# Two halves of the array's rows, a shared two-bank PSUM tile and earlier inputs in the edge networks of a graph kernel

## Chip, cores and metric

One Trainium2 chip; the kernel is one program on one of its cores. The metric is device time in microseconds (us) of one execution; lower is better. Engines are named as in the profile: PE (TensorE, matrix products into PSUM), PEld (its weight loads), DVE (VectorE), ACT (ScalarE), POOL (GpSimd, here mostly indirect DMAs), SP (issues DMAs).

## The reference

Two graph layers run one after the other on 6250 nodes of 160 values (64 scalars and 32 vectors of three) and 200000 edges, sorted by destination. Each layer is followed by a residual addition and a layer norm. Per edge a small network gives weights, which multiply the features of the edge's source node and the edge's own four values; the products are summed at the destination. Layer 1 (`i == 0` in the kernel):

```python
weight = silu(edge_attr_10 @ W_fc1) @ W_fc2          # 10 -> 100 -> 192 per edge
w0, w1, w2, w3 = weight[:, :64], weight[:, 64:128], weight[:, 128:160], weight[:, 160:]
gs, gv = x1s[src], x1v[src]                           # gathered source nodes
mid0a = w0 * gs * e_s
mid0b = w3 * (einsum('euc,ec->eu', gv, e_v) / SQRT3)
mid1a = w1[:, :, None] * gs[:, :, None] * e_v[:, None, :]
mid1b = w2[:, :, None] * gv * e_s[:, :, None]
agg = segment_sum(concatenate([mid0a, mid0b, mid1a, mid1b]), dst, n) / 4
```

Layer 2 (`i == 1`) is of the same kind: `hid = silu(edge_attr_64 @ fc_w1 / 8)` (64 -> 64), `w = hid @ fc_w2 / 8` (64 -> 224), five products instead of four, the same sum by destination, then linear mixes, gates and the norm. All is float32.

## The kernel before

**Tiles, units, chunks.** The 200000 edges are 1563 tiles of 128 edges (edges on partitions). Four tiles are a unit (391 of them), two tiles a pair. Because the edges are sorted, consecutive tiles fall into a narrow window of nodes: `plan()` makes 284 groups of 3 to 12 tiles whose destinations lie within 32 nodes (W).

**One unit** of `windows(i, ...)`, called once per layer, goes through these steps at different times:

- `gather(p)`: POOL gathers the source rows of the layer's node table by indirect DMA, one per tile (L665), four units ahead, into tile `g` (8 buffers of a pair).
- `inputs(c)`: SP loads the edge attributes of a chunk, features on partitions. In layer 1 a chunk is one unit: 10 partitions by 512 edges (L598) into one of three tiles `e0`, `e1`, `e2` that were zeroed once, so that a product may read all 128 partitions. In layer 2 a chunk is two units, and the 512 edges of a unit stand as two blocks of 64 partitions by 256 edges, one under the other (L607), in tile `e` (2 buffers). An input is asked for where the first product needs it in program order; SP's queue runs ahead as far as the buffers allow.
- `hidden(u)`: the first product of the edge network into PSUM tile `pa` (one buffer of one bank), then Silu by ACT into tile `h` in SBUF. Layer 1: one product, 128 rows by 100 columns of weights, 512 edges streamed (L623, L624). Layer 2: `fc1[1]` holds the 64x64 weights twice on the diagonal, so one product streams 256 columns for 512 edges (L634, L636).
- `weights(p)`: the second product, per tile, into `pw` (three banks, a pair in each): layer 1 with 100 rows, layer 2 with 64 rows, the upper half for the unit's first pair and the lower half for its second (L656). Pair by pair.
- `places(p)`: DVE makes the selection matrices `sel` (node in the window equals the edge's destination, times the four edge values; L699). `products(p)`: DVE multiplies `pw` with `g` into `mid` (L681, L686).
- `aggregate(t)`: six (layer 1) or seven (layer 2) products with `sel` as weights sum the tile's edges into `pg` (two banks, one per group in work), in the four 32-column tiles of the array (L723). At a group's end ACT copies `pg` to `r` (L728, L730).
- `turn(g)`: a unit later TensorE turns `r` into PSUM tile `pt` (one bank; L737 to L744), and DVE adds `pt` into the running sums `sm` (L749) and `sr` (L751) at the window's offset, which it reads from a table (L746).

**Order.** The loop at L783 writes out, for step u: gather(u+4), weights(u+2), hidden(u+3), places and products(u+2), then aggregate for the four tiles of u, then turn for the groups that ended in step u-1, then a piece of the node work (`second_nodes`, `last_nodes`, in PSUM tile `pn`). TensorE's products keep this program order (`keep_in_program_order`, helpers at L134 and L139, whose lines stand for all products in the profile); other engines' queues are ordered by the scheduler, which also sets the semaphores from the tiles that instructions read and write. `issue_after` ties the offset's read to the last DVE selection.

**PSUM.** All eight banks are used: pw 3, pg 2, pa 1, pn 1, pt 1. The prologue (`turn_nodes`, `send_nodes`, `checked`) borrows the same tiles. `general()` is a branch for inputs that aren't as the plan expects; it doesn't run here.

A float32 product appears in the profile as two LDWEIGHTS and two MATMUL instructions.

Of the kernel before, what the change touches and what calls it, by code (L numbers as in the profile page):

```python
# [81 lines left out]
def edges_of(t):  # L82
    return min(P, E - t * P)
# [3 lines left out]
def kernel(ctx: ExitStack, tc: tile.TileContext, a, out):  # L87
# [25 lines left out]

    tail_n, tail_e = N - (NB - 1) * P, E - (NT - 1) * P
# [85 lines left out]
    nc.gpsimd.dma_start(fc1[0][:10], a["W_fc1"])  # L200
# [115 lines left out]
    def checked():  # L316
        p = psum.tile([P, 512], F32, name="pa", bufs=1)
# [228 lines left out]
    def windows(i, loads, work):  # L546
# [13 lines left out]
        ec = (EC // 2, EC)[i]  # L560

        inputs_of = None
        if i == 0:

            inputs_of = [loads.tile([P, EC * P // 2], F32, name=f"e{k}", bufs=1) for k in range(3)]
            for e in inputs_of:
                nc.vector.memset(e, 0.0)
# [24 lines left out]
        def inputs(c):  # L592

            e0 = c * ec * P
            n = min(ec * P, E - e0)
            if i == 0:
                e = inputs_of[c % 3]
                nc.sync.dma_start(e[:10, :n], a["e10"][:, e0:e0 + n])  # L598
            else:

                e = loads.tile([P, EC * P // 2], F32, name="e", bufs=2)
                for u in range(0, n, 4 * P):
                    for h in range(2):
                        r = u + h * 2 * P
                        m = min(2 * P, n - r)
                        if m > 0:
                            nc.sync.dma_start(e[h * 64:h * 64 + 64, u // 2:u // 2 + m],  # L607
                                              a["e64"][:, e0 + r:e0 + r + m])
            made["e", c] = e

        def hidden(u):

            t0 = 4 * u
            c = t0 // ec
            if ("e", c) not in made:
                inputs(c)
            e = made["e", c]
            n = min(4 * P, E - t0 * P)
            p = psum.tile([P, 512], F32, name="pa", bufs=1)
            h = work.tile([P, 512], F32, name="h", bufs=2)  # L620
            at = (t0 % ec) * P
            if i == 0:
                matmul(p[:100, :n], fc1[0], e[:, at:at + n], start=True, stop=True)  # L623
                nc.scalar.activation(h[:100, :n], p[:100, :n], AF.Silu)  # L624
            else:
                at //= 2
                k = P if n > 2 * P else 64
                m = min(n, 2 * P)
# [4 lines left out]
                for kk, c0, c1 in parts:  # L633
                    matmul(p[:kk, c0:c1], fc1[1][:kk, :kk], e[:kk, at + c0:at + c1],  # L634
                                     start=True, stop=True)
# [3 lines left out]
        def weights(p):  # L639

            pw = psum.tile([P, 512], F32, name="pw", bufs=3)
            q = pw.rearrange("p (j d) -> p j d", j=2)
            h = made["h", p // 2]
            for j in range(2):
                t = 2 * p + j
                if t >= NT:
                    break
                n = edges_of(t)
                if i == 0:
                    l = h[:100, (t % 4) * P:(t % 4) * P + n]  # L650
                    r = fc2[0]
                else:
                    k = 64 * (p % 2)
                    l = h[k:k + 64, j * P:j * P + n]
                    r = fc2[1][k:k + 64, :]
                matmul(q[:n, j, :nw], l, r, start=True, stop=True)  # L656
            made["w", p] = q
# [75 lines left out]
        def turn(g):  # L733
            r = made["r", g]
            pt = psum.tile([P, 512], F32, name="pt", bufs=1)
# [47 lines left out]
        for u in range(-4, units + 1):  # L783
# [6 lines left out]
            if 0 <= u + 2 < units:  # L790
                for p in pairs_of(u + 2):
                    weights(p)
# [26 lines left out]
    def general(i, loads, work):  # L819
# [18 lines left out]
        def body(t, n):  # L838
# [20 lines left out]
            ph = psum.tile([P, 512], F32, name="pa", bufs=1)  # L859
# [7 lines left out]
            pr = psum.tile([P, 512], F32, name="pa", bufs=1)  # L867
# [122 lines left out]
```

## Time and profile before

| | |
|---|---|
| median of 8 runs | 6534.62 us (6483.35 to 6542.86) |
| the profiled execution: its own time | 6519.48 us |
| its span, first to last instruction | 6517.7 us |
| mean granted TensorE clock | 0.767 |
| PE / PEld instructions | 53817 / 53817 |
| layer 1's edge loop, first to last pw product | about 74 to 3277 us |
| layer 2's edge loop | about 3306 to 6495 us |

The costliest groups touched by the change, from the page's list (count, busy us, mean ns of one, idle time of the engine before it and what ended most of that):

| group | count | busy us | mean ns | idle before |
|---|---|---|---|---|
| POOL gathers, L665 | 3126 | 3014.7 | 964 | 3433.7, most for DVE mid |
| PE pg (sums) | 40638 | 1733.4 | 272 | 830.8, most "issue" |
| PE pw (second products) | 6252 | 1575.8 | 456 | 146.2 |
| PE pa (first products) | 1566 | 928.6 | 683 | 17.4 |
| ACT Silu, layer 1 (L624) | 391 | 232.8 | 595 | 1335.3 |
| ACT Silu, layer 2 (L636) | 392 | 150.1 | 383 | 1616.4 |
| DVE adds into sm (L749) | 568 | 162.7 | 287 | 1183.1 |

How to read it: busy time is a union of an engine's instructions, so overlapping products count once. "Issue" is time in which the engine waited for nothing that the profile shows. The chain of waits follows the last instruction back through whatever released each step. The granted clock is what the throttle let TensorE have; in this trace each piece of it is either 1.0 or 0.5.

### The profile page before, as it was taken

The numbers are of one execution on the slowest core, as the hardware profiler recorded it, in microseconds if no ns is written. First come the engines' busy times: TensorE is split into PE (matmuls) and PEld (weight loads), VectorE is DVE, ScalarE is ACT, GpSimd is POOL, SyncE is SP. The second block draws the span as 40 slices with busy tenths as digits, with TensorE's granted clock in tenths as the row PEclk, the third lists the DMA queues.
The fourth block names the chain that finished last, engine by engine and source line by source line (L and its number), as shares of the span: only waits on it lengthen the run. The fifth ranks groups of instructions, "written<-read, shape, count | busy, mean of one in ns | idle before, by whom it ended". The sixth has DMA issues, their size and how long they took to land.

```text
span 6517.7 us, 137335 instructions
## 1 busy us (share of the span) xinstructions
PE 4854.0 (74%) x53817; PEld 3253.8 (50%) x53817; DVE 2937.9 (45%) x10845; ACT 947.4 (15%) x2386; POOL 3036.3 (47%) x3232
## 2 busy tenths in 40 slices
PE   6787777777777777777767777777777777776766
PEld 4455555555555555555544444444444454444544
DVE  5544444444444444334344444444444444544444
ACT  1111111111111122111110000101111111111112
POOL 4555555444444344333345555555444444444443
PEclk8888888887887788777677777777777777777667
DMA  3222222222222122111122222222222222222221
GB/s 98 51 54 54 53 55 54 51 51 51 51 52 52 45 51 51 44 41 45 42 55 64 64 63 66 65 65 66 64 63 62 64 65 64 66 59 58 54 59 45
DMA packets 301526, 371.47 MB, mean 57 GB/s; under 512 B 86988, under 2 KB 245213, under 8 KB 300873
## 3 DMA queue, kind: packets, MB, share of 16 engines
q0 software_dynamic: 151056, 257.36, 16.3%
q1 hardware_dynamic: 121192, 88.36, 5.2%
q10 hardware_dynamic: 28624, 16.88, 0.9%
q8 instruction: 430, 7.05, 0.5%
q14 instruction: 224, 1.83, 0.1%
HBM read 341.49 MB, written 20.80 MB: 56 GB/s over the span
## 4 chain that ended last, share of the span: by engine, by line
PE 71%; issue 18%; another core or an unknown queue 5%; DVE 4%; ACT 1%; DVEq 0%; DMA 0%; SPq 0%; ACTq 0%
PE pg L134 24%; PE pw L134 23%; PE pa L134 12%; PE pn L134 7%; PE pt L139 4%; DVE sel L699 1%; PE pt L134 1%; DVE mid L686 1%; PE pn L139 1%; DVE mid L681 1%; DVE sm L749 0%; DVEq L746 0%; DVE nx L442 0%; DVE sr L751 0%
## 5 line engine op out<-in xcount | busy, mean ns | idle before, releaser
L665 POOL DMA_INDIRECT g<-table,src x3126 | 3014.7, 964 | 3433.7 <-DVE mid L686 2044.1
L134 PE MATMUL pg<-mid,sel 128*32 128x32 f32 (+3 forms) x40638 | 1733.4, 272 | 830.8 <-issue 813.9
L134 PEld LDWEIGHTS pg<-mid,sel 128*32 128x32 f32 x40638 | 1198.4, 127 | 1787.0 <-issue 1767.7
L134 PE MATMUL pw<-fc,h 100*128 100x192 f32 (+1 forms) x6252 | 1575.8, 456 | 146.2 <-issue 115.2
L699 DVE SCALAR_TENSOR_TENSOR sel<-iota,off,ea 128x128 f32<-128x128 f32 x3126 | 958.4, 344 | 1441.0 <-remote 494.7
L134 PEld LDWEIGHTS pw<-fc,h 100*128 100x128 f32 (+1 forms) x6252 | 1153.5, 248 | 353.5 <-issue 257.9
L686 DVE TENSOR_TENSOR mid<-g,pw 128x192 f32<-128x192 f32 x3910 | 1167.4, 345 | 0.0
L134 PE MATMUL pa<-e,fc 128*100 128x512 f32 (+1 forms) x1566 | 928.6, 683 | 17.4 <-issue 10.3
L681 DVE TENSOR_TENSOR mid<-pw,g 128x256 f32<-128x256 f32 x1564 | 654.3, 418 | 597.6 <-PE pw L134 351.4
L749 DVE TENSOR_TENSOR sm<-pt,sm 96x128 f32 (+1 forms) x568 | 162.7, 287 | 1183.1 <-PE pt L139 650.2
L134 PEld LDWEIGHTS pa<-e,fc 128*100 128x100 f32 (+1 forms) x1566 | 328.9, 236 | 198.6 <-issue 190.6
L624 ACT ACTIVATE h<-pa 100x512 f32<-100x512 f32 x391 | 232.8, 595 | 1335.3 <-PE pa L134 1012.0
L728 ACT ACTIVATE r<-pg 128x96 f32<-128x96 f32 (+1 forms) x568 | 156.4, 275 | 1616.3 <-remote 623.1
L636 ACT ACTIVATE h<-pa 128x256 f32<-128x256 f32 x392 | 150.1, 383 | 1616.4 <-PE pa L134 1494.4
L139 PE MATMUL pt<-ident,r 128*96 128x128 f32 (+1 forms) x852 | 247.0, 310 | 101.6 <-DVE sr L751 56.0
L134 PE MATMUL pn<-rm,sm 96*128 96x128 f32 (+4 forms) x980 | 224.6, 400 | 107.7 <-DVE sm L749 93.3
L134 PE MATMUL pt<-ident,r 128*32 128x32 f32 x2272 | 151.3, 219 | 177.9 <-issue 122.8
L134 PEld LDWEIGHTS pn<-rm,sm 96*128 96x128 f32 (+3 forms) x980 | 215.0, 288 | 122.1 <-DVE sm L749 97.4
L134 PEld LDWEIGHTS pt<-ident,r 128*32 128x32 f32 x2272 | 111.1, 125 | 219.5 <-issue 176.7
L139 PEld LDWEIGHTS pt<-ident,r 128*96 128x96 f32 (+1 forms) x852 | 111.4, 131 | 204.0 <-issue 104.4
L139 PE MATMUL pn<-ident,nx 128*128 128x128 f32 (+1 forms) x196 | 50.6, 348 | 140.0 <-DVE nx L442 140.0
L134 PE MATMUL pn<-rr,sr 64*128 64x128 f32 (+2 forms) x196 | 79.7, 502 | 65.9 <-DVE sr L751 57.2
(132 smaller groups left out, 1359.7 us busy)
## 6 DMA issues: line engine op xcount, KB each, us to landing
g<-table,src POOLq DMA_INDIRECT x3126
e<-in_e SPq DMA_DIRECT2D x781, 64.0 KB
e<-in_e SPq DMA_DIRECT2D x390, 20.0 KB
ea<-in_ea_main SPq DMA_DIRECT2D x63, 96.0 KB
xself<-no ACTq DMA_DIRECT2D x48, 96.0 KB
no<-xself SPq DMA_DIRECT2D x48, 96.0 KB
xg<-in_x_main SPq DMA_DIRECT2D x12, 320.0 KB
table<-rg SPq DMA_DIRECT2D x12, 320.0 KB
```

The source lines that it names most:

```text
L134: r = nc.tensor.matmul(*args, **kw)
L139: r = nc.tensor.transpose(*args)
L624: nc.scalar.activation(h[:100, :n], p[:100, :n], AF.Silu)
L636: nc.scalar.activation(h[:kk, c0:c1], p[:kk, c0:c1], AF.Silu, scale=0.125)
L665: nc.gpsimd.indirect_dma_start(out=g[:n, j, :], out_offset=None, in_=table[i][:, :], in_offset=bass.IndirectOffsetOnAxis(ap=of(t)[0], axis=0))
L681: nc.vector.tensor_tensor(two, q[:n, :m, 0:2 * S].rearrange("p j (k d) -> p j k d", k=2), gs, OP.mult)
L686: nc.vector.tensor_tensor(o[:, :, at:at + 96].rearrange("p j (c d) -> p j c d", c=3), gv, q[:n, :m, None, w0:w0 + V].to_broadcast([n, m, 3 ...
L699: made["last"] = nc.vector.scalar_tensor_tensor(s[:n, j], iota[:n, None, :].to_broadcast([n, 4, W]), w, e[:, :, None].to_broadcast([n, 4, ...
L728: nc.scalar.activation(r[:, :w], pg[:, :w], AF.Copy)
L749: nc.vector.tensor_tensor(sm[:h, :, at], pt[:h, :P].rearrange("p (c w) -> p c w", c=4), sm[:h, :, at], OP.add)
```

## The change

- **Layer 1's first products** become two: the unit's edges stand as two blocks of 10 partitions by 256 edges, at partitions 0 and 64, as in layer 2. `fc1[0]` holds the 10 rows of weights at both places, and each half of 64 rows multiplies its own block into its own bank. ACT then runs two Silu.
- **Layer 2's second products** are issued alternately from the unit's two pairs (`weights(ps)` takes both pairs at once), so that the row halves alternate. Layer 1 keeps its order; both pairs' PSUM tiles are taken before the first product.
- **One PSUM tile `pair`** of two banks, made once, replaces pa and pt. Columns 0 to 255 of the banks hold first products (layer 1: both banks; layer 2: bank `u % 2`); columns 256 to 511 of bank `g % 2` hold the turned sums of group g. The prologue's uses of pa and pt go to its two banks.
- **Inputs**: both layers use chunks of two units and the same three zeroed tiles, now made outside `windows`; `hidden` asks for its own chunk and the next. Layer 1's full chunks are loaded by one transfer per half.

```diff
+    pair = psum.tile([P, 2, 512], F32, name="pair", bufs=1)
...
-    nc.gpsimd.dma_start(fc1[0][:10], a["W_fc1"])
+    for r in (0, 64):
+        nc.gpsimd.dma_start(fc1[0][r:r + 10], a["W_fc1"])
...
-        z = psum.tile([P, 512], F32, name="pa", bufs=1)
+        z = pair[:, 0, 0:P]
...
-            tag, k = (("pg", 2), ("pn", 1), ("pg", 2), ("pt", 1))[j]
-            p = psum.tile([P, 512], F32, name=tag, bufs=k)
+            tag, k = (("pg", 2), ("pn", 1), ("pg", 2), (None, 0))[j]
+            p = psum.tile([P, 512], F32, name=tag, bufs=k) if tag else pair[:, 1]
...
         def inputs(c):
...
+            e0 = c * EC * P
+            n = min(EC * P, E - e0)
+            k, of_e = ((10, a["e10"]), (64, a["e64"]))[i]
+            e = inputs_of[c % 3]
+
+            for h in range(2):
+                if i == 0 and n == EC * P:
+                    nc.sync.dma_start(
+                        e[h * 64:h * 64 + k].rearrange("p (u m) -> p u m", m=2 * P),
+                        of_e[:, e0:e0 + n].rearrange("p (u h m) -> p u h m", h=2, m=2 * P)[:, :, h])
+                    continue
                 for u in range(0, n, 4 * P):
...
         def hidden(u):
 
             t0 = 4 * u
-            c = t0 // ec
-            if ("e", c) not in made:
-                inputs(c)
+            c = t0 // EC
+            for k in (c, c + 1):
+                if ("e", k) not in made and k * EC < NT:
+                    inputs(k)
             e = made["e", c]
             n = min(4 * P, E - t0 * P)
-            p = psum.tile([P, 512], F32, name="pa", bufs=1)
             h = work.tile([P, 512], F32, name="h", bufs=2)
-            at = (t0 % ec) * P
+            at = (t0 % EC) * P // 2
+            m = min(n, 2 * P)
             if i == 0:
-                matmul(p[:100, :n], fc1[0], e[:, at:at + n], start=True, stop=True)
-                nc.scalar.activation(h[:100, :n], p[:100, :n], AF.Silu)
+
+                halves = [(0, m)] + [(1, n - m)] * (n > m)
+                for j, m in halves:
+                    k = slice(64 * j, 64 * j + 64)
+                    matmul(pair[:100, j, :m], fc1[0][k], e[k, at:at + m], start=True, stop=True)
+                for j, m in halves:
+                    nc.scalar.activation(h[:100, 2 * P * j:2 * P * j + m], pair[:100, j, :m], AF.Silu)
             else:
-                at //= 2
+                p = pair[:, u % 2]
...
-        def weights(p):
-
-            pw = psum.tile([P, 512], F32, name="pw", bufs=3)
...
+        def weights(ps):
+
+            for p in ps:
+                pw = psum.tile([P, 512], F32, name="pw", bufs=3)
+                made["w", p] = pw.rearrange("p (j d) -> p j d", j=2)
+
+            for p, j in [(p, j) for p in ps for j in range(2)] if i == 0 else \
+                    [(p, j) for j in range(2) for p in ps]:
                 t = 2 * p + j
...
+                if t < NT:
+                    h, n = made["h", p // 2], edges_of(t)
+                    if i == 0:
+                        l, r = h[:100, (t % 4) * P:(t % 4) * P + n], fc2[0]
+                    else:
+                        k = slice(64 * (p % 2), 64 * (p % 2) + 64)
+                        l, r = h[k, j * P:j * P + n], fc2[1][k]
+                    matmul(made["w", p][:n, j, :nw], l, r, start=True, stop=True)
...
         def turn(g):
             r = made["r", g]
-            pt = psum.tile([P, 512], F32, name="pt", bufs=1)
+            pt = pair[:, g % 2, 2 * P:]
...
             if 0 <= u + 2 < units:
-                for p in pairs_of(u + 2):
-                    weights(p)
+                weights(pairs_of(u + 2))
...
+            inputs_of = [loads.tile([P, EC * P // 2], F32, name=f"e{k}", bufs=1) for k in range(3)]
+            for e in inputs_of:
+                nc.vector.memset(e, 0.0)
             for i in range(2):
-                windows(i, loads, work)
+                windows(i, loads, work, inputs_of)
```

More of the change, by code (lines that the diff above doesn't have):

```diff
@@ L316, in checked @@
     def checked():
-        p = psum.tile([P, 512], F32, name="pa", bufs=1)
+        p = pair[:, 0]
         transpose(p[:1, :P], over, ident)
@@ L543, in last_nodes, with windows @@
         return [fetch], [summed]
-    def windows(i, loads, work):
+    def windows(i, loads, work, inputs_of):
         nw = (192, 224)[i]
@@ L559, in windows @@
         made = {}
[L560 to L567, printed above, removed]
         def scalars(c):
@@ L592, in inputs @@
         def inputs(c):
[L594 to L601, printed above, removed]
-                for u in range(0, n, 4 * P):
[L603 to L608, printed above, removed]
+            e0 = c * EC * P
[8 more added lines that the diff above has]
+                    continue
+                for u in range(0, n, 4 * P):
+                    r = u + h * 2 * P
+                    m = min(2 * P, n - r)
+                    if m > 0:
+                        nc.sync.dma_start(e[h * 64:h * 64 + k, u // 2:u // 2 + m],
+                                          of_e[:, e0 + r:e0 + r + m])
             made["e", c] = e
@@ L613, in hidden @@
             t0 = 4 * u
-            c = t0 // ec
-            if ("e", c) not in made:
-                inputs(c)
+            c = t0 // EC
+            for k in (c, c + 1):
+                if ("e", k) not in made and k * EC < NT:
+                    inputs(k)
             e = made["e", c]
             n = min(4 * P, E - t0 * P)
-            p = psum.tile([P, 512], F32, name="pa", bufs=1)
             h = work.tile([P, 512], F32, name="h", bufs=2)
-            at = (t0 % ec) * P
+            at = (t0 % EC) * P // 2
+            m = min(n, 2 * P)
             if i == 0:
-                matmul(p[:100, :n], fc1[0], e[:, at:at + n], start=True, stop=True)
-                nc.scalar.activation(h[:100, :n], p[:100, :n], AF.Silu)
+                halves = [(0, m)] + [(1, n - m)] * (n > m)
[4 more added lines that the diff above has]
+                    nc.scalar.activation(h[:100, 2 * P * j:2 * P * j + m], pair[:100, j, :m], AF.Silu)
             else:
-                at //= 2
+                p = pair[:, u % 2]
                 k = P if n > 2 * P else 64
-                m = min(n, 2 * P)
                 if n == 4 * P or n <= 2 * P:
@@ L634, in hidden @@
                     matmul(p[:kk, c0:c1], fc1[1][:kk, :kk], e[:kk, at + c0:at + c1],
-                                     start=True, stop=True)
+                           start=True, stop=True)
                     nc.scalar.activation(h[:kk, c0:c1], p[:kk, c0:c1], AF.Silu, scale=0.125)
             made["h", u] = h
-        def weights(p):
-            pw = psum.tile([P, 512], F32, name="pw", bufs=3)
-            q = pw.rearrange("p (j d) -> p j d", j=2)
-            h = made["h", p // 2]
-            for j in range(2):
-                t = 2 * p + j
[L646 to L657, printed above, removed]
+        def weights(ps):
[4 more added lines that the diff above has]
+                    [(p, j) for j in range(2) for p in ps]:
+                t = 2 * p + j
+                if t < NT:
[6 more added lines that the diff above has]
+                    matmul(made["w", p][:n, j, :nw], l, r, start=True, stop=True)
         def gather(p):
@@ L858, in body @@
                 in_offset=bass.IndirectOffsetOnAxis(ap=s[:n, 0, :], axis=0))
-            ph = psum.tile([P, 512], F32, name="pa", bufs=1)
+            ph = psum.tile([P, 512], F32, name="pn", bufs=1)
             nc.tensor.matmul(ph[:hid, :n], fc1[i][:parts, :hid], e[:parts, :n],
@@ L865, in body @@
             nc.tensor.matmul(pw[:n, :nw], h[:hid, :n], fc2[i][:hid, :nw], start=True, stop=True)
-            pr = psum.tile([P, 512], F32, name="pa", bufs=1)
+            pr = psum.tile([P, 512], F32, name="pn", bufs=1)
             nc.tensor.matmul(pr[:n, :n], dstf[:n].to_broadcast([n, n]), ident[:n, :n],
```

## The prediction

> **What bounds the kernel now.** First the page's busy shares and its chain of waits.
>
> ```profile
> span 6517.7 us, 137335 instructions
> ...
> PE 4854.0 (74%) x53817; PEld 3253.8 (50%) x53817; DVE 2937.9 (45%) x10845; ACT 947.4 (15%) x2386; POOL 3036.3 (47%) x3232
> ...
> PE 71%; issue 18%; another core or an unknown queue 5%; DVE 4%; ACT 1%; DVEq 0%; DMA 0%; SPq 0%; ACTq 0%
> PE pg L134 24%; PE pw L134 23%; PE pa L134 12%; PE pn L134 7%; PE pt L139 4%; DVE sel L699 1%; PE pt L134 1%; DVE mid L686 1%; PE pn L139 1%; DVE mid L681 1%; DVE sm L749 0%; DVEq L746 0%; DVE nx L442 0%; DVE sr L751 0%
> ```
>
> The chain is 71% matmuls and 18% "issue" (TensorE between its own instructions), so about 0.89 of a microsecond taken from TensorE should reach the end. pa (hidden products), pw (edge weights) and pt (turned sums) are what the change touches.
>
> Second, the busy times cut at the two layers, whose edge loops I take from the first and last pw product of each form.
>
> ```profile
> core 0: us, PE busy (x) PEld busy (x) DVE busy (x) ACT busy (x) POOL busy (x), PEclk, DMA share, GB/s
> 74.00:3277.00 3203.00, 2479.74 (x24499) 1656.81 (x24500) 1379.22 (x4993) 520.09 (x1372) 1493.71 (x1559) 0.79 0.20 50
> ...
> 3306.00:6495.00 3189.00, 2295.57 (x28608) 1539.28 (x28608) 1489.77 (x5600) 388.66 (x904) 1516.25 (x1563) 0.74 0.25 62
> ```
>
> Each layer has 391 units of four tiles: 8.19 us and 8.16 us a unit. Layer 2 has 184 us less TensorE work, a lower granted clock, and the same length: a warning that TensorE's time is not passed on whole.
>
> **The hidden products of layer 1.** Third, the same two windows with the instructions that touch pa alone.
>
> ```profile
> 74.00:3277.00 3203.00, 554.50 (x780) 173.36 (x780) 0.00 (x0) 232.17 (x390) 0.79 0.20 50
> 3306.00:6495.00 3189.00, 370.85 (x782) 154.61 (x782) 0.00 (x0) 149.72 (x391) 0.74 0.25 62
> ```
>
> A float32 product is two instructions. Layer 1 streams 512 columns per unit (554.5/390 = 1.42 us), layer 2 streams 256 (370.9/391 = 0.95 us). After the change layer 1 has two products of 256 columns in different halves of the rows. If they run side by side, their cost is layer 2's row: 554.5 - 370.9 = 184 us saved. That halves can run side by side is seen in layer 2's weights, both times at a granted clock of 1.00:
>
> ```profile
> 5004.74 1.03 PE L134 MATMUL pw<-fc,h 64*128 64x224 f32 x8
> ...
> 3353.30 1.84 PE L134 MATMUL pw<-fc,h 64*128 64x224 f32 x8
> ```
>
> The upper unit runs its eight instructions as four simultaneous pairs (starts 13 ns apart), the lower one almost one after another. Bounds for layer 1: 0 (no overlap) to 184; I take 184, because these products follow 16 long pw instructions, behind which they can queue. Layer 1 gets a change of tile shape between pw (all rows) and pa (half the rows); layer 2's pa row already holds such a change on either side.
>
> Two Silu instead of one: 383 ns each (149.7/391) against 595 (232.2/390) is 0.17 us x 390 = 67 us of ScalarE, which is 15% busy. The reader of h is the next unit's pw, behind four tiles of sums; without that cover the edit costs 67. I take 0, since half of h is ready earlier than all of it was.
>
> **Layer 2's weights, interleaved.** I classed all 390 units by the starts of their eight instructions: 164 run as four pairs, 226 have three pairs or fewer. In those the second tile pair's first instruction starts 0.6 us or more after the first (0.61 at 3353.30), while its PSUM buffer had been free at the unit's start in 333 of 385 (from the end of the product that last read it). So it is late because it is eighth in the stream; interleaved it is fourth. Bounds: 0 to 226 x 0.81 (1.84 - 1.03) = 183 us. I take half the distance, 0.4 us: 90 us. The Trainium skill, "TensorE: Matmul & The Clock Gate", Part 3, says that matmuls start and end strictly in program order. By that rule no unit could have paired before, and the edit would gain 390 x 0.81 = 316 us; the row at 5004.74 contradicts it.
>
> **Two halves for the turned sums.** With one pt buffer a second turn waits for the VectorE adds of the first:
>
> ```profile
>   PE pt L139: 56.0, 23
>   PE pt L134: 29.0, 16
> ```
>
> (from the view of line 751, who waited for it). Bounds 0 to 85; I take 60, since some of these turns would meet another wait at once.
>
> Relief so far: 184 + 90 + 60 = 334, times 0.89 = 297 us.
>
> **What the change adds.** *A wait.* pt now lies in the banks of pa. In the changed program's instruction list 220 first hidden products of layer 1 and 221 of layer 2 wait for VectorE, where there was no such wait: the turn before them must be added into sr (L751) first. Queued behind this wait are the hidden product and all four tiles of sums; ScalarE waits for the former, VectorE's selections for the latter. Whether the adds are in time is in the trace: for each I compare its end with the start of the next pa product. In layer 1, 106 of 284 end later, by 166 us together; in layer 2, 109 of 277, by 157. An example, the add 4.8 us after the product that would now wait for it:
>
> ```profile
> 971.40 1.02 PE L134 MATMUL pa<-e,fc 128*100 128x512 f32 x2
> ...
> 975.78 0.28 DVE L749 TENSOR_TENSOR sm<-pt,sm 96x128 f32 x1
> ...
> 975.98 0.17 DVE L751 TENSOR_TENSOR sr<-pt,sr 64x32 f32 x1
> ```
>
> Together 323 us, scaled to the 441 waits (x 441/561) 254; TensorE did work in only 265 of the 323 us, so the loss is at most 265 x 0.79 = 208. The bottom is 0: a TensorE that waits lets VectorE (45% busy) catch up. I take half, 104. The Trainium skill, "PSUM — Partial Sum Buffer", section "PSUM bank collisions raise a hardware error", says that two engines may not touch one bank in the same 32 partitions at once, even at other columns. By that rule the wait cannot be dropped; by the addresses alone (columns 0 to 255 against 256 to 511) it need not exist and the sum would be 104 us lower. No row of this trace tells between them.
>
> *Instructions.* One product more per unit of layer 1 is two loads and two products, 1560 on top of 48999. TensorE's idle time before pg put down to "issue" is 257.2 us in layer 1 and 556.8 in layer 2, 5 and 10 ns per instruction of the layer: 8 to 16 us; I take 12.
>
> *The clock.* Busy share and clock of the two layers above: 0.774 and 0.79, 0.720 and 0.74, a slope of about 0.9. Removing 184 + 30 us from layer 1's 2480, with about 110 off its length, gives 0.733, a clock 0.036 lower, 4.5% of 2270: 100 us. Layer 2 with 120 off 2296 and 50 off its length gives 0.693, clock -0.025, 3.4% of 2176: 73 us. A slower clock itself raises the busy share, so these are tops: 0 to 173. I take 100.
>
> **Edits I cost at nothing.** Layer 1's inputs are 10 rows in two halves: 392 issues of 20 KB against 390, each with twice as many pieces of half the size; asked for one chunk ahead, into three buffers whose last reader is two chunks back. The pa products wait for such a DMA under 6 us in all, so there is little to gain; without the cover (8 us per unit against the 1.5 us that the first e transfer takes in the chain, at 68.11) a chunk would cost 1.5 us, 196 x 1.5 = 294 us, but asking earlier cannot uncover it. SP's queue holds the same issues in nearly the same order. Layer 2 loses its own input tiles and must wait for layer 1's last chunk: 0 to 3 us, beside the 29 us between the layers. One more small load on POOL's queue in the prologue lies in a 40 us idle stretch of POOL. Prologue tiles moved to the pair keep separate banks.
>
> **Sum.** 6519 (profiled execution: span 6517.7, its own time 6519.5) - 297 + 104 + 12 + 100 = 6438. The median of the runs, 6534.6, lies 15 above the profiled one: 6453, rounded to **6450**.
>
> **Rivals.**
> *The shared bank decides.* Relief less clock and instructions is 297 - 100 - 12 = 185 us; if the 441 new waits cost over 185/441 = 0.42 us each, the change is slower. At the full 254 us with only layer 1's relief and the turns (244 x 0.89 = 217) and clock 100: 6535 - 217 + 254 + 12 + 100 = **6684**; from there down to 6570. For: 38% of the adds are late, and late by 1.5 us on average. Against: most late ones fall in stretches where TensorE itself trickles. 0.27.
> *TensorE's time is not what counts.* For: the layers' equal length despite 184 us less work; POOL's four gathers per unit take 4 x (0.96 + 0.30) = 5.0 us and the stalls called "issue" grow from 257 to 557 where TensorE has less to do. Then relief turns into issue time: **6535**, give or take 35. 0.21.
> *The halves don't overlap in layer 1.* 128-row weights before and column tiles behind could force order. Then 0 for 184, 150 x 0.89 = 134 relief, 104 + 12 lost, clock 40: 6535 + 22 = **6557**. Against: layer 2's pairs. 0.05.
> *No cost shows.* Waits and clock near 0 and pairing whole: (184 + 183 + 60) x 0.89 = 380, less 12: **6167** up to 6300. 0.09.
> The forecast, 6300 to 6500, has 0.38.
>
> **How the numbers follow.** A measurement here tells about 0.5% from no change, 33 us: 6502 to 6567. Faster: 0.36 of the forecast, 0.09, and 0.04 each from the first two rivals: 0.53. Same: 0.02 of the forecast, 0.13 of the second, 0.03 of the third: 0.18. Slower: the rest, 0.29. The range leaves out half of the best case and the top of the shared-bank case: **6250 to 6640**; the forecast's own is 6300 to 6500.
>
> **What would show it.** In the changed profile: layer 1's pa near 0.95 us per unit (371 us in all) with pairs of equal starts; layer 2's pw near 620 us instead of 709; waits of the hidden product for DVE sr, near 100 us in all; no pt waits for sr; PEclk near 0.76 and 0.72. I am wrong in the size if the clock holds, and in the sign if hidden products wait over 200 us for sr, or if "issue" grows by what pa loses.

## The result, and the profile after

The changed kernel is slower: 6724.81 us (6691.44 to 6741.69, 16 runs) against 6522.37 us for the kernel before on the same chip (46 runs), a ratio of 1.0307 [1.0288, 1.0326]. The profiled execution has a span of 6727.6 us and a mean granted clock of 0.733. Its page, busy shares and chain of waits:

```profile
span 6727.6 us, 139326 instructions
...
PE 4830.9 (72%) x54599; PEld 3285.7 (49%) x54599; DVE 2950.4 (44%) x10845; ACT 982.5 (15%) x2779; POOL 3035.8 (45%) x3233
...
PE 65%; issue 19%; another core or an unknown queue 8%; DVE 7%; ACT 1%; DVEq 1%; DMA 0%; SPq 0%; ACTq 0%
```

TensorE's busy time fell by 23 us while the span grew by 210; on the chain its share is smaller (71% before) and DVE and the unknown queue hold more. Busy times of the two layers' edge loops after:

```profile
82.00:3354.00 3272.00, 2447.99 (x25284) 1709.20 (x25284) 1390.04 (x5000) 549.03 (x1764) 1488.17 (x1559) 0.74 0.20 49
3386.00:6705.00 3319.00, 2299.67 (x28612) 1515.90 (x28612) 1492.40 (x5601) 392.38 (x904) 1521.32 (x1563) 0.73 0.24 60
```

(The second number is the length, the first with a count TensorE's busy time, then PEld, DVE, ACT, POOL; the clock follows.) Layer 1 is 69 us longer, layer 2 130; the other 11 are in the prologue and between the layers. Now the groups of instructions that the change made, and the waits of products (us in all, times, longest):

```profile
L137 PE MATMUL pw<-fc,h 64*128 64x224 f32 x3124 | 655.0, 490 | 47.6 <-issue 39.1 <-ACT h L639 2.2 <-DVE mid L687 0.7
L137 PE MATMUL pair<-e,fc 128*128 128x256 f32 x780 | 387.5, 590 | 135.2 <-DVE sr L752 115.9 <-issue 12.2 <-DVE nx L446 3.0
L137 PE MATMUL pair<-e,fc 64*100 64x256 f32 x1562 | 384.2, 565 | 195.6 <-DVE sr L752 178.9 <-DVE sel L700 5.9 <-DMA e<-in_e 5.2
```

```profile
PE pg L137 <- issue: 676.3, 1156, 3.3
...
PE pair L137 <- DVE sr L752: 350.6, 196, 5.7
```

The halves of layer 1 look as hoped: 384.2 us instead of 554.5. But in front of the same products 178.9 us of waiting for VectorE's add of the turned sums have appeared, and 115.9 in layer 2. The table puts the layers side by side; idle time is that in which TensorE ran neither a product nor a weight load, sorted by what ended it.

| us | layer 1 before | after | layer 2 before | after |
|---|---|---|---|---|
| length | 3203 | 3272 | 3189 | 3319 |
| granted clock | 0.787 | 0.738 | 0.744 | 0.727 |
| idle, ended by DVE | 94 | 363 | 61 | 240 |
| of that before hidden products | 0 | 187 | 0 | 124 |
| idle by issue | 377 | 284 | 739 | 729 |

In two of the five batches of experiments every kernel, the one before too, ran at about 4120 to 4180 us with few issue gaps, instead of 6250 to 6900; the expectations call this a chip of the second kind, though one chip number showed both, and ratios are compared within a batch only.

### The profile page after: what moved, and what is told of

Read it like the earlier page. It is cut to its first block, busy times and chain, and to the rows that moved or that the text cites. A ratio compares the mean times of both kernels' runs of the same rounds, so it can differ in the third digit from the quotient of the medians.

```text
span 6727.6 us, 139326 instructions
## 1 busy us (share of the span) xinstructions
PE 4830.9 (72%) x54599; PEld 3285.7 (49%) x54599; DVE 2950.4 (44%) x10845; ACT 982.5 (15%) x2779; POOL 3035.8 (45%) x3233
## 4 chain that ended last, share of the span: by engine, by line
PE 65%; issue 19%; another core or an unknown queue 8%; DVE 7%; ACT 1%; DVEq 1%; DMA 0%; SPq 0%; ACTq 0%
PE pg L137 23%; PE pw L137 20%; PE pair L137 11%; PE pn L137 7%; PE pair L142 4%; DVE sel L700 2%; DVE mid L687 2%; PE pn L142 1%; DVE mid L682 1%; DVE sm L750 1%; DVE sr L752 1%; DVEq L747 0%; DVE nx L446 0%; DVE rg L277 0%
## 5 line engine op out<-in xcount | busy, mean ns | idle before, releaser
L137 PE MATMUL pg<-mid,sel 128*32 128x64 f32 (+4 forms) x40638 | 1800.8, 286 | 685.9 <-issue 676.3
L137 PE MATMUL pair<-e,fc 64*100 64x256 f32 (+1 forms) x2348 | 772.7, 573 | 331.0 <-DVE sr L752 294.8
L750 DVE TENSOR_TENSOR sm<-pair,sm 96x128 f32 (+1 forms) x568 | 163.6, 288 | 1474.9 <-PE pair L142 519.2
L137 PEld LDWEIGHTS pair<-e,fc 64*100 64x100 f32 (+1 forms) x2348 | 300.4, 230 | 646.2 <-DVE sr L752 383.9
L628 ACT ACTIVATE h<-pair 100x256 f32<-100x256 f32 x782 | 257.5, 381 | 1412.9 <-PE pair L137 1179.0
L639 ACT ACTIVATE h<-pair 128x256 f32<-128x256 f32 x392 | 150.4, 384 | 1622.6 <-PE pair L137 1563.5
L142 PE MATMUL pair<-ident,r 128*96 128x128 f32 (+1 forms) x852 | 255.3, 321 | 144.8 <-DVE sr L752 68.7
L137 PE MATMUL pair<-ident,r 128*32 128x32 f32 x2272 | 170.7, 223 | 240.6 <-issue 178.8
L137 PEld LDWEIGHTS pair<-ident,r 128*32 128x32 f32 x2272 | 113.8, 126 | 275.0 <-issue 204.8
L142 PEld LDWEIGHTS pair<-ident,r 128*96 128x96 f32 (+1 forms) x852 | 114.2, 134 | 273.7 <-issue 140.2
```

The source lines that it names most:

```text
L137: r = nc.tensor.matmul(*args, **kw)
L142: r = nc.tensor.transpose(*args)
L628: nc.scalar.activation(h[:100, 2 * P * j:2 * P * j + m], pair[:100, j, :m], AF.Silu)
L639: nc.scalar.activation(h[:kk, c0:c1], p[:kk, c0:c1], AF.Silu, scale=0.125)
L750: nc.vector.tensor_tensor(sm[:h, :, at], pt[:h, :P].rearrange("p (c w) -> p c w", c=4), sm[:h, :, at], OP.add)
```

## Experiments

Each ratio is to the kernel before, run in the same batch. The kernel before had 6519.58 us in batch 1, 4133.32 in batch 2, 6683.74 in batch 3, 4133.93 in batch 4 and 6650.70 in batch 5.

### The shared tile alone

The kernel before, with hidden products and turned sums in the two banks of one tile: in layer 2 in both banks as in the change, in layer 1 a bank for each.

```diff
+    pair = psum.tile([P, 2, 512], F32, name="pair", bufs=1)
-            p = psum.tile([P, 512], F32, name="pa", bufs=1)
+            p = pair[:, u % 2 if i else 0]
-            pt = psum.tile([P, 512], F32, name="pt", bufs=1)
+            pt = pair[:, g % 2, 2 * P:] if i else pair[:, 1]
```

> The kernel before with the pair of banks shared in layer 2 alone: hidden products in columns 0 to 255 and turned sums in columns 256 onwards of the two banks; layer 1 keeps its 512-column hidden product in one bank and its turned sums in the other, and inputs, weights and halves are as before. Only layer 2 can change. Theory A (the new wait decides): about 200 us more idle time of TensorE and weight loads ended by VectorE in layer 2 (61 in the kernel before, 240 in the changed one), and a time of 6620 to 6720. Theory B (the loss comes from the clock or the halves, not from the wait): 6500 to 6560. The prediction's own term for this wait, about half of 104: 6570 to 6590.

Measured: 6734.19, ratio 1.0329 [1.0290, 1.0368], 215 us more: as much as the whole change. But not in layer 2 alone. Layer 1, whose hidden products and turned sums have a bank each, grew from 3203 to 3297 us (layer 2 from 3189 to 3289). Busy times of the two layers, and the waits of products in layer 1:

```profile
81.00:3378.00 3297.00, 2461.98 (x24499) 1626.31 (x24500) 1386.28 (x4995) 523.70 (x1373) 1486.52 (x1559) 0.79 0.20 49
3409.00:6698.00 3289.00, 2356.49 (x28619) 1603.00 (x28623) 1490.20 (x5602) 391.78 (x904) 1523.12 (x1563) 0.71 0.24 61
```

```profile
PE pair L135 <- DVE sr L752: 203.5, 103, 6.1
PE pg L135 <- issue: 169.4, 306, 1.8
...
PE pair L140 <- DVE sr L752: 71.0, 23, 5.2
```

The first of these waits should not exist if banks mattered: hidden products in bank 0 wait for adds that read bank 1. Of layer 1's hidden products 222 wait for VectorE's semaphore there, one in the kernel before. The wait is set by the tile, not by the bank: both lie in one tile, and semaphores are made from tiles. Layer 2 did what theory A expected of it: idle time ended by VectorE grew from 61 to 253 us and the layer by 100, the low end. Most of the rest of the 215 comes from layer 1 (94), which no expectation had. The clock tells the two layers apart: layer 1 kept it (0.786), layer 2's fell from 0.744 to 0.714 though its products are those of the kernel before.

### Two tiles instead of one

The changed kernel, with the same two banks as two tiles, and layer 2's turned sums in the bank that the next hidden product doesn't use.

```diff
-    pair = psum.tile([P, 2, 512], F32, name="pair", bufs=1)
+    pair = [psum.tile([P, 512], F32, name=f"pair{k}", bufs=1) for k in range(2)]
...
-            pt = pair[:, g % 2, 2 * P:]
+            pt = pair[(made["u"] + 1) % 2 if i else g % 2][:, 2 * P:]
```

> The changed kernel with its two banks as two tiles of one bank each instead of one tile of two, and in layer 2 the turned sums in the bank that the next hidden product doesn't use. By the instruction list no hidden product of layer 2 waits for VectorE any more (221 in the changed kernel); the 221 of layer 1, whose two halves use both tiles, stay. Theory A (the wait on the shared tile is the loss): layer 2's idle time ended by VectorE falls from 240 us to about the 61 of the kernel before, layer 2 gets 120 to 200 us shorter (3319 to about 3150), layer 1 stays within 40 us of 3272; time 6520 to 6620. Theory B (what the wait took is taken by something else: issue, clock): the waits vanish but layer 2 stays over 3270; time 6680 to 6740.

The batch ran at 4130 us: 4136.56, ratio 1.0004 [0.9992, 1.0015], which decides nothing about the changed kernel, so it was run again beside it.

> The changed kernel again, beside the next three on one chip. The runs so far fall on two chips: on one the kernel before takes 6520 us, with TensorE idle by issue for 1116 us in the two layers, on the other 4133 us with hardly any. If this call is on a chip of the first kind: 6690 to 6740 (ratio 1.03). If on one of the second kind: theory A (the wait on the shared tile) says that the two-tile version there, at 4137 with 71 us of hidden products waiting for VectorE in layer 1, gets layer 2's waits on top, 50 to 100 us: 4180 to 4240 (ratio 1.01 to 1.025). Theory B (the loss belongs to TensorE's own trickle): no difference there, 4120 to 4150.

> The changed kernel with its two banks as two tiles, so that no hidden product of layer 2 waits for VectorE. On a chip of the first kind (before at 6520): theory A 6520 to 6620, layer 2 at about 3150 and its idle time ended by VectorE near 61; theory B 6680 to 6740. On one of the second kind: 4137 again.

Measured in batch 3: the changed kernel 6887.32, 1.0309 [1.0228, 1.0391]; two tiles 6773.20, 1.0134 [1.0052, 1.0215]. Waits of layer 2's products, the changed kernel first, then two tiles:

```profile
PE pg L137 <- issue: 497.0, 787, 2.6
PE pair L137 <- DVE sr L752: 225.8, 102, 5.7
```

```profile
PE pg L137 <- issue: 630.0, 1020, 3.3
...
PE pair L137 <- DVE sr L752: 47.0, 19, 5.7
```

The wait went from 225.8 to 47.0 (the rest is turned sums waiting for turned sums), and issue before the sums took 133 back. Layer 2's idle time ended by VectorE fell by 189 us (287 to 98), its length by 64 (3366 to 3302). Layer 1 lost 33: its hidden products kept most of their wait (147 us of 170), its turned sums lost theirs, and idle time ended by VectorE fell from 348 to 258. So the shared tile costs, and about a third of what a wait took comes back when it goes. Taken as ratios to the 6520 that the expectation started from, theory A had 1.000 to 1.015 and theory B 1.025 to 1.034: the time is at A's upper end. Of the 1.3% that stay, layer 1's remaining waits have a part; how large, no run tells. This run moved the turned sums to another bank too, so that tile and bank are told apart by `b_share2` alone.

### Turns before the sums

The same move in the changed kernel and in the kernel before.

```diff
+                for g in ended:
+                    turn(g)
+                    turned_to = g + 1
                 for t in range(4 * u, min(4 * u + 4, NT)):
...
-                for g in ended:
-                    turn(g)
-                    turned_to = g + 1
```

> The changed kernel with one move: the turns of the groups that ended in the step before are issued before the step's four tiles of sums instead of behind them. Instructions, banks and waits stay the same; only the distance between a turn (and its VectorE add) and the next hidden product, which waits for that add, grows by the four tiles of sums (about 4 us). The changed kernel has a median of 6725, 202 above the kernel before. Theory A (the new wait for the VectorE add in the shared bank decides): TensorE and weight-load idle time ended by VectorE falls from about 600 us (363 + 240 by layer) to under 200, the granted clock stays near 0.73 to 0.75, and the time falls by most of what is freed: 6300 to 6520, with 6420 the likeliest. Theory B (TensorE's time is not what counts; the clock or the stalls called issue fill whatever is freed): the idle time ended by VectorE falls the same way, but issue grows or the clock falls by as much, and the time is 6690 to 6740. Theory C (the VectorE adds are late because TensorE itself trickles, so more room in program order changes little): the idle time ended by VectorE stays over 450 us and the time is 6650 to 6740.

> The kernel before with the same move of the turns ahead of the step's sums (control for the run above). Here a hidden product doesn't wait for the turn's add, so theory A (shared bank) and theory B expect no difference: 6490 to 6560. If the move has a value or a cost of its own (a turn that waits for ScalarE's copy of its sums, a selection order on VectorE that changes), it is seen here as a difference of more than 35 us and has to be taken off the run above.

Measured: the changed kernel 6548.39, ratio 1.0031 [1.0001, 1.0062]; the kernel before 6262.82, ratio 0.9586 [0.9549, 0.9623] (batch 3: 6395.40, 0.9568 [0.9492, 0.9644]). The control moved most, against both theories. In the changed kernel the idle time ended by VectorE went from 603 to 35 us, as theory A had it, but the time stayed above A's range, and the control's own gain, which was to be taken off, is the larger one (4.1% against 2.8): this run doesn't price the wait. For the shared tile brought another one. The changed kernel's waits of products with early turns:

```profile
PE pair L142 <- ACT h L628: 301.3, 224, 4.9
PE pair L137 <- ACT h L639: 232.2, 235, 5.4
```

Now the turn follows the hidden product and waits until ScalarE has read that from the same tile. In the kernel before no hidden product is in the way, and VectorE stops standing in front of turned sums that come late. VectorE's waits in the kernel before, then with early turns:

```profile
DVE sm L749 <- PE pt L139: 650.2, 153, 8.1
DVE sel L699 <- remote: 494.7, 160, 21.6
DVE sel L699 <- PE pt L139: 416.8, 123, 7.1
```

```profile
DVE sel L699 <- remote: 960.5, 282, 21.5
...
DVE sm L749 <- PE pt L139: 109.3, 128, 1.2
...
DVE sel L699 <- PE pt L139: 27.6, 10, 3.7
```

The adds (sm, L749) waited 650.2 us for turned sums and selections 416.8 us; both nearly vanish, while selections wait longer for something that the profile doesn't name ("remote"). In layer 1 TensorE's busy time fell from 2480 to 2378 us at a clock of 0.808 instead of 0.787; idle time ended by DVE or an unknown queue fell from 244 to 65 in layer 1 and 88 to 3 in layer 2, with 172 us more of waits for ScalarE. That the gain comes from these waits is read from the profiles; no run separates it. This is the fastest version in batches 1 and 3, and it has nothing of the change.

> The kernel before with early turns alone. On a chip of the first kind: 6263 again. On one of the second kind: the early turns with the group's own bank and a second hidden bank took 4144 against 4133 there, so 4120 to 4150: nothing to gain where TensorE doesn't wait for the node work.

### Interleaved weights alone

The kernel before with the new `weights(ps)`, which goes through a unit by `j` and then by pair in layer 2.

```diff
-                for p in pairs_of(u + 2):
-                    weights(p)
+                weights(pairs_of(u + 2))
```

> The kernel before with one part of the change alone: in layer 2 the weights of a unit are issued alternating between the two row halves. The prediction's step: 90 us less of pw time in layer 2 (709 to about 620), times 0.89, so 6440 to 6460 (bounds 6360 to 6525). In the changed kernel pw of layer 2 measured 655.0, which taken alone is 54 us less: 6475. Theory B (TensorE's time is not what counts): pw falls but issue or the clock takes it back, 6500 to 6545.

Measured: 6517.97, ratio 0.9997 [0.9971, 1.0022]. pw of layer 2 fell from 709.0 to 683.5 us, layer 2's issue from 739 to 769: no gain that can be seen, as theory B said.

### Layer 1's halves, without any shared tile

`best1` is the changed kernel with early turns, two tiles for hidden products alone and the turned sums behind the sums of their own group; `best1_whole` is the same with layer 1's hidden product whole and its inputs in chunks of one unit, as in the kernel before. The first part of the diff belongs to both, the second to `best1_whole`.

```diff
-            pt = pair[:, g % 2, 2 * P:]
+            pt = made["p", g][:, 2 * P:]
...
-                for j, m in halves:
-                    k = slice(64 * j, 64 * j + 64)
-                    matmul(pair[j][:100, :m], fc1[0][k], e[k, at:at + m], start=True, stop=True)
+                matmul(pair[u % 2][:100, :n], fc1[0], e[:, :n], start=True, stop=True)
```

> The changed kernel with two tiles for hidden products alone, turned sums in the group's own bank and early turns. On a chip of the first kind: 6160, range 6090 to 6220, if the halves of layer 1 pay on top of the early turns; 6230 to 6290 if a lower clock takes that back. On one of the second kind: 4160 again.

> The version with own tiles for the hidden products, turned sums in the group's bank and early turns, layer 1's hidden product whole. On a chip of the first kind (before at 6500 to 6700), where the version with halves measured 0.978 [0.970, 0.986] and its layer 1 3157 us at a clock of 0.746: ratio 0.955 to 0.97, clock of layer 1 at least 0.79 and layer 1 shorter than 3157 if the halves' lower clock costs more than they save; 0.985 to 1.0 if the halves save. On one of the second kind: 1.002 again.

Measured: with halves 6528.89, 0.9779 [0.9702, 0.9857] (batch 3), slower than any case expected; whole 6464.84, 0.9721 [0.9654, 0.9788] (batch 5), a little over the range expected. Layer 1 with halves, then whole:

```profile
72.00:3229.00 3157.00, 2484.90 (x25280) 1711.93 (x25280) 1393.34 (x4999) 551.88 (x1765) 1488.61 (x1560) 0.75 0.21 51
```

```profile
74.00:3183.00 3109.00, 2382.05 (x24501) 1608.87 (x24501) 1387.45 (x4995) 519.01 (x1373) 1498.65 (x1559) 0.81 0.21 52
```

With halves TensorE is busy 103 us longer, at a clock of 0.746 instead of 0.811. The hidden products alone, in the same order:

```profile
L137 PE MATMUL pair<-e,fc 64*100 64x256 f32 x1562 | 373.9, 540 | 13.4 <-issue 6.9 <-DMA e<-in_e 5.5
```

```profile
L137 PE MATMUL pair<-e,fc 128*100 128x512 f32 x780 | 529.2, 766 | 9.8 <-DMA e<-in_e 5.6 <-issue 3.6
```

155 us are saved there, and yet TensorE is busy 103 us longer: everything else in layer 1 took over 200 us more at the lower clock. The two batches differ by 0.5% in the kernel before, 16 us of such a layer, so of the 48 us some 30 stand in these profiles. The intervals of the two ratios overlap: a saving of up to some 30 us isn't excluded, one of 155 is. Batch 2 with halves had 1.0058 [1.0039, 1.0076], batch 4 whole 1.0022 [1.0010, 1.0035], layer 1 at 2015 and 2001 us.

> The changed kernel with two one-bank tiles that the hidden products have for themselves, the turned sums put behind the sums in the group's own bank (columns 256 onwards), and the turns issued before the step's sums. No hidden product waits for VectorE and no turn for a Silu. Against the kernel before with early turns alone (6263 measured) it has the halves of layer 1, alternating banks for hidden products and the interleaved weights. Prediction's terms for the halves: 184 us times 0.89, less 12 of instructions and half of the 100 of clock: 6263 - 164 + 62 = 6160, range 6090 to 6220. If the halves' gain is all taken back by a lower clock (layer 1 had 0.725 with halves and 0.808 without, both with early turns): 6230 to 6290. If the turn in the group's own bank costs a new wait: over 6290.

> The version with the hidden products' own two tiles, turned sums in the group's bank and early turns, measured at 0.978 of before on a chip of the first kind and 1.006 on one of the second, with layer 1's hidden product whole again (512 columns, one product, banks in turn). The difference is the halves of layer 1 alone. If the halves pay what their busy time says (132 us less occupancy): ratio 0.99 to 1.005 on the first kind. If the lower clock takes it back (weights, sums, node work and turns of layer 1 were 217 us longer with halves): ratio 0.955 to 0.975, layer 1 at a clock of 0.79 or more and shorter than the 3157 us with halves. On the second kind: 1.00 to 1.01.

Beside early turns alone in batch 3 (6395.40) the version with halves is 134 us slower (74 in the profiled executions). Layer 2 has a part of that: its weights fell from 723 to 669 us of busy time, but issue grew from 698 to 810. A further part may be a wait of its own: in batch 3 sums waited 115.9 us for adds out of their group's bank. `b_early_pg` has that placing in the kernel before, with whole hidden products and weights not interleaved:

> The kernel before with early turns, the turned sums in the group's own bank, and the freed bank given to the hidden products as a second buffer; layer 1's hidden product stays whole at 512 columns, weights and inputs stay as they were. Pair to the run above: the difference is the halves of layer 1 with the other small parts of the change. Expected 6240 to 6280, as the kernel before with early turns alone (6263), since no hidden product there waits for its bank; over 6300 if the group's own bank is a bad place for the turned sums, 6200 or less if a second bank for the hidden products is worth something by itself.

It had 4144.02, 1.0028 [1.0015, 1.0041], in batch 2; its price in a batch of the first kind stays open.

### Does the clock follow the rows in use?

> The kernel before itself, for a profile on the same chip as the next three. On a chip of the first kind: layer 1 near 3200 us at a clock of 0.787, idle by issue 377 us in layer 1 and 739 in layer 2. On one of the second kind: 4133 us with issue under 250 us in all.

```diff
-                matmul(p[:100, :n], fc1[0], e[:, at:at + n], start=True, stop=True)
+                matmul(p[:100, :n], fc1[0][:64], e[:64, at:at + n], start=True, stop=True)
```

> The kernel before with one edit: the hidden product of layer 1 uses 64 rows of the array instead of 128 (its inputs have 10 rows; the others are zero), still as one product of 512 columns, so it takes as long as before and nothing runs beside it. It asks why the halves lowered layer 1's granted clock (0.787 to 0.738, and 0.804 to 0.746 with early turns). Theory R (the clock follows the rows in use): the clock of layer 1 falls to 0.74 to 0.76 and layer 1 gets over 60 us longer, ratio 1.01 to 1.025. Theory T (the clock follows TensorE's busy time only, which stays): clock 0.78 to 0.80, ratio 0.995 to 1.005.

Measured in batch 4: 4182.22, ratio 1.0106 [1.0078, 1.0134]. Layer 1, in the kernel before as profiled in that batch, then with 64 rows:

```profile
73.00:2097.00 2024.00, 1819.64 (x24499) 1254.14 (x24500) 1396.91 (x4993) 520.99 (x1372) 1501.49 (x1559) 0.96 0.30 79
```

```profile
73.00:2195.00 2122.00, 1974.22 (x24499) 1290.83 (x24500) 1402.92 (x4993) 522.62 (x1373) 1500.75 (x1559) 0.91 0.28 75
```

The same 24499 products stream the same columns, TensorE's busy share rises from 0.90 to 0.93, and the clock falls from 0.956 to 0.910. Leaving out rows of zeros made the kernel slower, by 98 us in this profile, the slowest of five executions, and by 48 in the medians.

But the expectation's "takes as long as before" is wrong. One unit of each, the kernel before first, both at a granted clock of 1.00:

```profile
1000.08 0.81 PE L134 MATMUL pw<-fc,h 100*128 100x192 f32 x4
1000.73 1.02 PE L134 MATMUL pa<-e,fc 128*100 128x512 f32 x2
1001.68 0.59 PE L134 MATMUL pg<-mid,sel 128*32 128x160 f32 x19
```

```profile
1000.17 0.81 PE L134 MATMUL pw<-fc,h 100*128 100x192 f32 x4
1000.92 1.10 PE L134 MATMUL pa<-e,fc 64*100 64x512 f32 x2
1001.95 0.46 PE L134 MATMUL pg<-mid,sel 128*32 128x160 f32 x15
```

With 64 rows the hidden product starts 0.75 us after the first of these weights instead of 0.65, and the sums 1.78 us after it instead of 1.60. Over all units of layer 1 at full clock the median from the last weights instruction to the first sum is 1.285 us (339 units) instead of 1.116 (358): 0.17 us a unit, 66 in 391 units, for a product of another shape among products on more rows. That alone is as large as the loss in the medians.

The clock did fall beside it. Its pieces are multiples of 3.41 us in these traces. After such a stretch at half clock in which TensorE was busy throughout (over 97%), the full clock came back in 23 of 26 cases with 128 rows and in 25 of 82 with 64; at full clock, busy stretches kept it in both. So the busy share as the profile counts it doesn't set the clock alone. Whether the rows in use count is not shown: the time lost around the product, 0.25 us at half clock, is counted as busy and is 7% of a stretch, and in layer 1 of the kernel before's first profile stretches busy to 93 to 97% got the full clock back in only 7 of 19 cases. It was not repeated in a batch of the other kind, but the halves show a fall there (0.811 to 0.746).

### The rest

`b_turn_mid` (the kernel before, turns behind two of the four tiles of sums) leaves out the turned sums of the last four groups; `b_early_ahead` is the kernel before with early turns and the inputs asked for a chunk ahead.

> The kernel before with the turns issued behind two of the step's four tiles of sums (before: behind all four, 6520; ahead of all four: 6263). If the gain of the early turns comes from the adds being done before the node work that follows in program order (in layers 1 and 2 93 and 61 us of TensorE's idle time before node products ended by VectorE, and 120 of layer 1 from the queue that carries the selections, all of which fell to 5, 3 and 60), half the distance should keep most of it, and the turns' wait for ScalarE's copies (157 and 73 us with early turns) should shrink: 6230 to 6330. If the gain comes from the order of VectorE's work ahead of the sums, it is lost here: 6400 to 6520.

> The kernel before with early turns and the edge inputs asked for a chunk ahead into three buffers shared by both layers (a part of the change that no run has had alone). On a chip of the first kind pa waits for its inputs hardly at all: 0.955 to 0.96 as with early turns alone. On one of the second kind hidden products of the kernels without this part waited 92 to 118 us for their inputs: 0.975 to 0.99 if that is on the path, 0.995 to 1.0 if the gathers set the pace there.

Measured: 4122.84, 0.9976 [0.9964, 0.9988], in batch 2, and 4123.35, 0.9972 [0.9961, 0.9983], in batch 4. The first has no expectation for such a batch, and the best place of the turn in one of the first kind stays open; the second lies where the expectation put it if the gathers set the pace there, which no run shows. Earlier inputs did nothing for what they were for: TensorE's idle time before hidden products for their DMA in layer 1 is 88 us in the kernel before and 102 with them.

> The changed kernel. On a chip of the first kind: 1.031 a third time. On one of the second kind, where it has not been measured: the two-tile version there is at 1.000, with 71 us of hidden products of layer 1 waiting for VectorE; the shared tile adds layer 2's waits. Theory A (a wait costs wherever TensorE is close to the bound): 1.005 to 1.02. Theory B (the waits cost only beside the issue gaps): 0.998 to 1.003.

Batch 5: 6863.39, 1.0331 [1.0258, 1.0404]. The changed kernel was never run in a batch of the second kind, so whether it loses there is open.

## Why the prediction was wrong

- **Layer 1's halves (184 us).** Nearly right in size: 554.5 to 384.2 us of busy time, and 94% of the halves start within 40 ns of each other (7 ns in the median). From the last weights instruction to the first product behind the hidden one a unit took 1.12 us before and 0.87 after at full clock, 2.16 and 1.57 at half. At the mix of clocks before (188 units wholly at full clock, 113 at half) that is an estimated 150 us in 391 units. The change of tile shape, which the prediction put at nothing, takes 0.09 us of each unit at full clock: the hidden product starts 256 ns after the last weights instruction instead of 162.
- **Interleaved weights (90 us).** pw of layer 2 lost 54 us in the changed kernel and 26 by itself, and none of it is seen at the end.
- **Two halves for the turned sums (60 us).** Nothing. Turned sums waited 85.0 us for the adds before, and 68.7 plus 55.8 after: two banks in one tile are one buffer.
- **Times 0.89.** This factor assumed that what leaves TensorE's chain leaves the time. b_weights contradicts it in layer 2, where issue takes what is freed; there the rival "TensorE's time is not what counts" was right.
- **The wait (104 us, at most 208).** The step that failed most. The adds' lateness, counted in the trace before, was a good estimate and its half a bad one: b_share2 priced the shared tile at 215 us (189 to 240 by the interval), 0.49 for each of its 443 waits, beyond the turning point of 0.42. The thought behind the half, that VectorE catches up while TensorE waits, finds nothing in the runs: in the changed kernel hidden products idled 187 and 124 us for VectorE in the two layers, where 166 and 157 had been counted. The reason given was wrong as well: not banks but the one tile make the wait. Whether products and adds could use one bank at once, by separate tiles at other columns, was not tried.
- **Instructions (12 us).** Not seen; issue fell in layer 1. The second Silu, put at nothing, cost nothing that the runs show: idle time ended by ScalarE fell from 54 to 39 us in layer 1.
- **The clock (100 us, at most 173).** About right in size, but reasoned from the wrong thing. In layer 1 TensorE's busy time fell by 32 us (2480 to 2448) where the halves alone lost 170, so other products took some 140 us more; 0.787 to 0.738 on the other 1925 us is an estimated 130. This fall belongs to the halves: b_share2 has the waits without halves and keeps 0.786. Layer 2's fall, 0.744 to 0.727, belongs mostly to the shared tile, which alone brought 0.714, while the interleaved weights alone had 0.740; it is part of the 215 us. The slope of 0.9 was read off the rounded clocks and busy shares of two layers (with three digits it is 0.8); b_64rows shows a higher share with a lower clock.

The runs give a simpler sum: the shared tile alone cost 215 us, the interleaved weights alone nothing, and the halves with the clock that they bring saved at most some 30 us in `best1`. That is 6520 + 215 = 6735 against 6725 measured. The parts were measured beside different kernels, so that the closeness is partly luck. Of the rivals, "the shared bank decides" (6684, chance 0.27) came within 41 us, and its sign, over 200 us of hidden products waiting for sr, came true (178.9 and 115.9); its bank did not.

## What to carry to other kernels

Put two uses into one PSUM tile only if each may wait for the other: the dependency is taken from the tile, even across banks. Before a product is cut to fewer rows of the array, measure what the change of shape costs around it and what becomes of the clock of everything beside it; its own busy time tells neither. And look at where a step stands in the program order before changing its buffers: in the batches at 6500 to 6700 us, moving the turns by four tiles of sums gained 4%, which no buffer did. In those at 4130 us early turns were run only together with other edits, and no version there gained or lost more than about 1%.

## What was not expected of the hardware

- Using 64 instead of 128 rows for one product in every unit, most of them zeros, took 0.17 us a unit more at full clock and lowered the granted clock of the layer from 0.956 to 0.910 with TensorE busier than before.
- The kernel before took 4129.55 us in one batch and 6650.70 (median) in another. POOL and DVE are busy as long in both (layer 1: 1501 and 1397 us, against 1494 and 1379 in the first profile); what goes is issue (377 to 46 us in layer 1, 739 to 152 in layer 2) and with it the low clock (0.787 to 0.956). What sets this was not found.
